# Filling TensorE's pauses with unread products, moving biases and a rank step, in a six-stage float32 kernel

## The chip, the cores and the metric

The kernel runs on one core of one Trainium2 chip. The core has a matrix engine (TensorE, PE in the profile; its weight loads are PEld), a vector engine (DVE), a scalar engine (ACT), a general engine (POOL), and SP, which here issues DMAs. Each engine works through its own queue of instructions in order; engines wait for each other on semaphores. TensorE writes its products to PSUM, the other data lie in SBUF.

The metric is device time in microseconds. Before the change it is 1187.05 us, the median of three runs (1184.86 to 1189.95).

## The reference, cut to what matters

`x` is 2 x 64 x 1024 (128 rows, one for each SBUF partition); six stages each add their result to it, and each but the first stage's context reads a layer norm of `x`.

```python
x = x + xattn0(layernorm(x), ctx)      # q1 = fake_quant(x1), q2 = fake_quant(ctx); q1 @ q2
x = x + mamba(layernorm(x), ...)       # in_proj, causal conv of 4, SSM over 8 groups of 16 heads, gate, group RMS norm, out_proj
x = x + lora_ffn(layernorm(x), ...)    # base product + top-2 of 8 LoRA experts
x = x + graph(ctx, layernorm(x), ...)  # four space-filling orders of the points, windows of 10 neighbours, attention, two layers, conv3
x = x + (layernorm(x) @ (weight * block_mask).T)
x12 = layernorm(x) @ w12.T + b12       # the last stage
x1, x2 = split(x12, 2)
x = x + (silu(x1) * x2) @ w3.T + b3
```

The graph stage takes its points from the context (the first three features of 1024 positions). To sort them, four keys are made for each point (Morton and Hilbert order, each with the axes in two orders), and each point's rank among the 1024 keys is counted.

## The kernel before

All is written out as one program; the loops are Python loops.

**Attention and state-space stage** (`mamba`). `quant_attention` (L171) loads the context in four pieces, quantizes and multiplies them. The function's last step is handed back as `update`, which the layer norm (`layernorm`, L140) applies to each half of `x`. `transposed` (L156) turns the normed `h` into `hT` with eight TensorE transposes (L163), copied out by DVE for the first half and ACT for the second. From there `project` (L312 to L320) multiplies `hT` by chunks of `in_proj_w`: a load of up to four chunks (2 MB) on SP into one of three buffers, then 8 products a chunk (L319) into one of two PSUM tiles of pool `pin`.

The order of instructions on all engines is the order in which the code is written (`manual_schedule`). For each of eight groups `g` the loop (from L464) does: two projections of the main path, each followed by `conv` (ACT L325 and L328, DVE L334, ACT L335); two projections of the gate; in the second of them `decays` (products L384 and L392 in pool `ps`, two buffers, tag `misc`; DVE `gm` L386 and `mt` L396, ACT L395); `turned` (transposes L405, DVE `xs` L406); the first half of the out projection of the group before (`out_half`, L453); `mixed` (L417); the other half; `gated` (DVE L429 to L436), `accumulate` (L461). `rms` of a group (L440) stands behind the next group's first projection.

Between these, `side(n)` runs the next n steps of `point_ranks`, a generator that makes the sorting keys and ranks, mostly on DVE. Steps of its Hilbert loop (L635 to L650) are 17 small integer operations each; later steps are the comparisons L724 and L725. Group 0 runs one step after each of its two `conv` and two after each gate projection; groups from 1 on also run two after the first `out_half` and four after `accumulate`.

**LoRA stage** (`lora_experts`). A layer norm with the last group's `update`, transposes, the router product L524, the base product L528, then the experts; L566 is the last product.

**Graph stage** (`point_cloud`). Its preparation is not in a hand-written order. It loads small weights on SP (L760 to L766 for each of two layers), the biases of the last stage (L1083, L1084), the spread and the masked linear's weight `w_attn` (4 MB, L1253). Then an iteration for each of 88 sets of points, with PSUM pools `g_ps` (3 buffers of tag `misc`), `g_pa` (2, `sc`), `g_po` (2, `op`) and `g_pt` (1, `pt`): one PSUM bank each, eight in all. At its end conv3 (L1187) is summed in two `op` tiles, normed (L1200 to L1208), passed through a leaky ReLU (for the second half POOL L1210 makes 0.2 h, DVE L1214 takes the larger), and added to `x` (L1212, L1215).

**Last stage** (`masked_linear_and_ffn`). It opens PSUM pools of its own: four tiles `p12`, two `lo`, two `misc`. Four bias products (L1272: a row of 6 biases chosen by a column of the identity, 6 rows deep) start `p12`; then norm, transposes (`turn`, L1282), the masked linear into `lo` (L1276, 32 records of 512 columns), the sum with `x` (L1309), norm and transposes again, two bias products into new `lo` tiles, four products with w12 (64 records), ACT's SiLU (L1319) and DVE's product (L1321), transposes, and the product with w3 in two halves (2 x 16 records). The weights (three loads of 4 MB, L1266 and L1268) go out on SP when the graph stage's SBUF comes free. A float32 product appears as two records of TensorE.

Of the kernel before, what the change touches and what calls it, by code (L numbers as in the profile page):

```python
# [14 lines left out]
AF = mybir.ActivationFunctionType  # L15
ALU = mybir.AluOpType
# [4 lines left out]
P = 128  # L21
D = 1024
# [70 lines left out]
class Kernel:  # L93
# [46 lines left out]
    def layernorm(self, pool, tag="h", update=None):  # L140
# [13 lines left out]
        return h  # L154

    def transposed(self, pool, ps, h, tag="hT"):  # L156

        nc = self.nc
        hT = self.t(pool, [P, KC, P], tag=tag)
        for q in range(2):  # L160
            pt = self.t(ps, [P, 4, P], tag="misc")
            for j in range(4):
                nc.tensor.transpose(pt[:, j, :], h[:, (4 * q + j) * P:(4 * q + j + 1) * P], self.ident)  # L163
            if q == 0:
                nc.vector.tensor_copy(hT[:, 0:4, :], pt)
            else:
                nc.scalar.copy(hT[:, 4:8, :], pt)
        return hT
# [106 lines left out]
    def mamba(self):  # L275
# [3 lines left out]
        with ExitStack() as es:  # L279
# [7 lines left out]
            convw, convb, normw = self.convw, self.convb, self.normw  # L287

            h = self.layernorm(sb, update=update)
            hT = self.transposed(sb, ps, h)  # L290
# [13 lines left out]
            def side(n):  # L304
                for _ in range(n):
                    next(pieces, None)
# [157 lines left out]
            for g in range(G):  # L464
                cs, h0 = grp(g)
                st = dict(xc=self.t(gp, [P, CPG, P], tag="xc"), sg=self.t(gp, [P, CPG, P], tag="sg"), rl=[])
                for q in range(2):
                    rl = self.t(hp, [P, 8, S], tag="rl")
                    nc.gpsimd.tensor_tensor(rl, cm.unsqueeze(1).to_broadcast([P, 8, S]),
                                            dtT[:, 1, h0 + 8 * q:h0 + 8 * q + 8].unsqueeze(2).to_broadcast([P, 8, S]), ALU.mult)  # L470
                    st["rl"].append(rl)
                for q in range(2):
                    pt = project(17 + 16 * g + 4 * q, 4)
                    if q == 0 and prev:
                        rms(g - 1, prev)
                    conv(st["xc"][:, 4 * q:4 * q + 4, :], pt, CPG * g + 4 * q)
                    side(1)
                for q in range(2):
                    pt = project(25 + 16 * g + 4 * q, 4)
                    if q:  # L480
                        decays(g, st)
                    settle()
                    nc.scalar.activation(st["sg"][:, 4 * q:4 * q + 4, :], pt, AF.Silu)
                    side(2)
                if g == G - 2:
                    nc.sync.dma_start(self.w_ra, a["router_lora_a"])
                    nc.sync.dma_start(self.w_lb, a["lora_B"])
                turned(g, st)
                if prev:
                    out_half(g - 1, prev, 0)  # L490
                    side(2)
                mixed(g, st)
                if prev:
                    out_half(g - 1, prev, 1)
                gated(g, st)
                if prev:
                    accumulate(g - 1, prev)
                    side(4)
                prev = st
# [12 lines left out]
            def update(q, c):  # L512
                nc.vector.scalar_tensor_tensor(self.x[:, c], prev["po"][:, q, :], prev["rs"], self.x[:, c], ALU.mult, ALU.add)

            self.lora_experts(sb, ps, pout, update)

# [544 lines left out]
    def point_cloud(self):  # L1061
        nc, tc, a = self.nc, self.tc, self.a
        with ExitStack() as es:
            pool = lambda n, b, **k: es.enter_context(tc.tile_pool(name=n, bufs=b, **k))
            self.g_ps, self.g_pa = pool("g_ps", 3, space=PSUM), pool("g_pa", 2, space=PSUM)
# [15 lines left out]

            self.bias = self.t(self.g_win, [6, 512], tag="bias", bufs=1)
            nc.sync.dma_start(self.bias[0:4, :], a["L1_ffn_b12"].rearrange("a (q n) -> (a q) n", n=512))  # L1083
            nc.sync.dma_start(self.bias[4:6, :], a["L1_ffn_b3"].rearrange("a (q n) -> (a q) n", n=512))  # L1084
            self.ident16 = self.t(self.g_w, [P, P], BF16, tag="ident16")
# [100 lines left out]
            def part(q, r, w, v, start=False, stop=False):  # L1186
                nc.tensor.matmul(po[q][r, :], w, v[:, 512 * q:512 * q + 512], start=start, stop=stop, skip_group_check=True)  # L1187
# [8 lines left out]
            for q in range(2):  # L1196
                part(q, hi, w3b, phases[3]["out"], stop=True)
            st = self.t(self.g_hm, [P, 2, 6], tag="st3")
            for q in range(2):
# [9 lines left out]
            t3 = self.t(self.g_hm, [P, 512], tag="f11")  # L1209
            nc.gpsimd.tensor_scalar(t3, h[1], 0.2, None, ALU.mult)  # L1210
            nc.vector.scalar_tensor_tensor(h[0], h[0], 0.2, h[0], ALU.mult, ALU.max)
# [42 lines left out]


    def masked_linear_and_ffn(self):

        nc, tc, a = self.nc, self.tc, self.a
        with ExitStack() as es:
            sb = es.enter_context(tc.tile_pool(name="l_sb", bufs=1))  # L1260
            pp = es.enter_context(tc.tile_pool(name="l_po", bufs=1, space=PSUM))
            ps = es.enter_context(tc.tile_pool(name="l_ps", bufs=2, space=PSUM))
            es.enter_context(tc.manual_schedule(engines=ENGINES))
# [6 lines left out]

            def biased(po, j):
                nc.tensor.matmul(po, self.ident[0:6, j:j + 1].to_broadcast([6, P]), self.bias, start=True, stop=False)  # L1272

            def product(po, hT, w, n, kcs, biased):
# [3 lines left out]
            def turn(v, n):  # L1278

                pt = self.t(ps, [P, 4, P], tag="misc")  # L1280
                for j in range(4):
# [17 lines left out]

            p12 = [self.t(pp, [P, 512], tag=f"p12{j}") for j in range(4)]  # L1300
            for j in range(4):
                biased(p12[j], j)
            hT = normed(self.st)
            st = self.t(sb, [P, 2, 6], tag="st5")
            po = [self.t(pp, [P, 512], tag=f"lo{n}") for n in range(2)]
            for n in range(2):
                product(po[n], hT, self.w_attn, n, range(KC), False)
            for n in range(2):
                nc.vector.tensor_tensor(half(self.x, n), half(self.x, n), po[n], ALU.add)  # L1309
                nc.vector.bn_stats(st[:, n, :], half(self.x, n))  # L1310
            hT = normed(st)
            po = [self.t(pp, [P, 512], tag=f"lo{n}") for n in range(2)]
            for n in range(2):
                biased(po[n], 4 + n)
            act = self.t(sb, [P, D], tag="act")
# [7 lines left out]
            for n in range(2):  # L1323
                product(po[n], aT, w_3, n, range(4), True)
            aT.append(turn(act, 1))
            for n in range(2):
                product(po[n], aT, w_3, n, range(4, KC), True)
            for n in range(2):
# [67 lines left out]
```

## Time and profile before

| | |
|---|---|
| median of three runs | 1187.05 us (1184.86 to 1189.95) |
| the profiled execution | 1189.64 us, of which the span from first to last instruction is 1187.9 us |
| mean granted TensorE clock | 0.942 |
| DMA | 170.89 MB, mean 144 GB/s |
| stretch before the first projection, 41.62 to 47.77 us | PE busy 0.00 us |
| between `turned` and `mixed` of group 0, 116.34 to 122.90 us | PE busy 0.00 us |
| before the router, 484.92 to 490.60 us | PE busy 0.00 us |
| preparation of the graph stage, 512.24 to 554.20 us | PE busy 9.52 us |
| graph loop, 554.20 to 1102.06 us | PE busy 487.83 us |
| last stage from 1102.06 us | 85.8 us |

A profile is one execution taken by the hardware profiler. "Busy" is time in which an engine works on an instruction; for TensorE the clock that was granted (1.00 is full) is recorded as well. A wait names the instruction that waited, what released it, the total, how often, and the longest. In forty slices of 29.7 us each, the clock that TensorE was granted (in tenths, 9 is 0.9 or more) and the DMA engines' share:

```profile
PEclk9899899999999998875998989898999999999889
DMA  7777468686695757556011003010222000000640
```

The slices below full clock are spread over the run; the DMAs work mainly until 490 us, and again near the end.

### The profile page before, as it was taken

The numbers are of one execution on the slowest core, as the hardware profiler recorded it, in microseconds if no ns is written. First come the engines' busy times: TensorE is split into PE (matmuls) and PEld (weight loads), VectorE is DVE, ScalarE is ACT, GpSimd is POOL, SyncE is SP. The second block draws the span as 40 slices with busy tenths as digits, with TensorE's granted clock in tenths as the row PEclk, the third lists the DMA queues.
The fourth block names the chain that finished last, engine by engine and source line by source line (L and its number), as shares of the span: only waits on it lengthen the run. The fifth ranks groups of instructions, "written<-read, shape, count | busy, mean of one in ns | idle before, by whom it ended". The sixth has DMA issues, their size and how long they took to land.

```text
span 1187.9 us, 40798 instructions
## 1 busy us (share of the span) xinstructions
PE 1034.0 (87%) x18349; PEld 790.4 (67%) x18349; DVE 736.6 (62%) x1545; ACT 656.5 (55%) x1056; POOL 497.8 (42%) x404
## 2 busy tenths in 40 slices
PE   4699899999999998743887888888999989999998
PEld 1598869769678693432665666667778767777333
DVE  5688775767666755442554666666767568986311
ACT  4443326565664561014886788776777676776010
POOL 0010110101325145337877877685757658841000
PEclk9899899999999998875998989898999999999889
DMA  7777468686695757556011003010222000000640
GB/s 258 288 289 278 194 277 354 248 355 272 241 417 198 328 231 227 185 200 93 14 23 25 15 12 66 17 35 9 39 37 38 10 11 11 10 4 3 244 180 18
DMA packets 47888, 170.89 MB, mean 144 GB/s; under 512 B 26409, under 2 KB 27349, under 8 KB 40801
## 3 DMA queue, kind: packets, MB, share of 16 engines
q1 hardware_dynamic: 37704, 151.22, 34.3%
q10 hardware_dynamic: 3864, 12.82, 3.2%
q0 software_dynamic: 6144, 4.24, 1.9%
q8 instruction: 144, 2.36, 0.8%
q14 instruction: 32, 0.25, 0.1%
HBM read 163.05 MB, written 2.72 MB: 140 GB/s over the span
## 4 chain that ended last, share of the span: by engine, by line
PE 57%; DVE 18%; ACT 9%; issue 6%; POOL 6%; DMA 3%; SPq 1%; another core or an unknown queue 0%; ACTq 0%; DVEq 0%; POOLq 0%
PE misc L953 12%; PE pin L319 11%; PE po L453 7%; PE op L968 5%; DVE cpre L334 3%; PE sc L918 3%; POOL x L886 3%; ACT df L725 3%; PE p L1276 3%; PE lo L1276 2%; PE pt L978 2%; DVE df L724 2%; POOL e L936 2%; PE sc L927 1%; DMA ow<-in_ctx 1%
## 5 line engine op out<-in xcount | busy, mean ns | idle before, releaser
L319 PEld LDWEIGHTS pin<-hT,w 128*128 128x128 f32 x2320 | 264.6, 194 | 3.5 <-issue 3.0
L319 PE MATMUL pin<-hT,w 128*128 128x128 f32 x2320 | 266.4, 278 | 0.1
L953 PE MATMUL misc<-wz,xz 128*64 128x64 bf16 (+1 forms) x8256 | 211.2, 212 | 13.7 <-issue 9.6
L953 PEld LDWEIGHTS <-xz 128*64 128x64 f16 x8256 | 196.4, 115 | 30.5 <-issue 26.8
L886 POOL TENSOR_TENSOR x<-win,cen 128x960 f16<-128x960 f32 x88 | 171.0, 1949 | 66.3 <-PE sc L918 31.1
L955 ACT COPY u<-misc 128x512 f32<-128x512 f32 x258 | 148.8, 587 | 54.8 <-PE misc L953 29.3
L854 POOL DMA_INDIRECT sl<-src,place x128 | 129.0, 1007 | 44.7 <-issue 18.7
L909 ACT COPY xz<-x 64x1024 f16<-64x1024 f16 (+1 forms) x132 | 134.7, 1020 | 6.4 <-POOL x L886 3.4
L940 DVE STREAM_TRANSPOSE at<-e 128x512 f32<-128x512 f32 x88 | 61.4, 698 | 110.1 <-POOL e L936 110.0
L433 POOL TENSOR_TENSOR xc<-y,normw 128x512 f32<-128x512 f32 x8 | 8.3, 1038 | 279.7 <-DVE y L431 230.5
L936 POOL TENSOR_TENSOR e<-e,z 128x512 f32<-128x512 f32 x88 | 94.5, 1074 | 71.7 <-DVE z L935 63.8
L725 ACT ACTIVATE df<-df,neg 128x1024 f32<-128x1024 f32 x64 | 73.4, 1147 | 89.8 <-DVE df L724 85.3
L453 PE MATMUL po<-ow,xc 128*128 128x512 f32 x256 | 115.4, 604 | 1.9 <-DVE acc L461 1.4
L968 PE MATMUL op<-u,at 128*32 128x64 f32 (+1 forms) x2752 | 93.8, 255 | 22.3 <-issue 13.4
L334 DVE SCALAR_TENSOR_TENSOR cpre<-craw,convw,cpre 128x126 f32<-128x126 f32 (+2 forms) x240 | 78.1, 347 | 29.1 <-ACT cpre L328 23.4
L968 PEld LDWEIGHTS op<-u,at 128*32 128x32 f32 x2752 | 64.5, 112 | 39.8 <-issue 21.8
L918 PEld LDWEIGHTS <-xz 128*64 128x64 f16 x2752 | 54.6, 113 | 49.1 <-issue 48.4
L453 PEld LDWEIGHTS po<-ow,xc 128*128 128x128 f32 x256 | 48.1, 193 | 58.1 <-issue 55.4
L724 DVE SCALAR_TENSOR_TENSOR df<-hi_r,hl,lo_r 128x1024 f32<-128x1024 f32 x64 | 81.7, 1303 | 4.0 <-DMA lo_r<-rows 2.8
L708 POOL DMA_INDIRECT place<-cst,rank x64 | 66.1, 1033 | 40.1 <-issue 15.3
L918 PE MATMUL sc<-x,xz 128*64 128x32 f16 x2752 | 66.6, 186 | 6.4 <-issue 6.4
L970 ACT COPY oT<-op 128x256 f32<-128x256 f32 (+1 forms) x88 | 41.4, 471 | 54.4 <-PE op L968 48.4
(319 smaller groups left out, 1400.3 us busy)
## 6 DMA issues: line engine op xcount, KB each, us to landing
w<-in_in_proj_w SPq DMA_DIRECT2D x36, 2048.0 KB
ow<-in_out_proj_w SPq DMA_DIRECT2D x16, 2048.0 KB
w<-in_L_ffn_w SPq DMA_DIRECT2D x3, 4096.0 KB
ow<-in_ctx SPq DMA_DIRECT2D x8, 1024.0 KB
hi_r<-rows ACTq DMA_DIRECT2D x8, 512.0 KB
lo_r<-rows ACTq DMA_DIRECT2D x8, 512.0 KB
df<-in_L_attn_mask ACTq DMA_DIRECT2D x8, 512.0 KB
w<-in_base_W SPq DMA_DIRECT2D x2, 2048.0 KB
```

The lines of the kernel that those rows point to most:

```text
L319: nc.tensor.matmul(pt[:, c, :], w[:, c, kc, :], hT[:, kc, :], start=(kc == 0), stop=(kc == KC - 1))
L334: nc.vector.scalar_tensor_tensor(pv[:, :, s:], rv[:, :, :S - s], convw[:, cc + c, 3 - s:4 - s], pv[:, :, s:], ALU.mult, ALU.add)
L453: nc.tensor.matmul(st["po"][:, n, :], st["xc"][:, 4 * q + c, :], ow[:, c, 512 * n:512 * n + 512], start=(q == 0 and c == 0), stop=(q == 1 ...
L725: nc.scalar.activation(df, df, AF.Sign, bias=neg[:, cc:cc + 1], scale=1.0, accum_out=sums[:, c:c + 1])
L854: nc.gpsimd.indirect_dma_start(out=ph[c][:, m, :], out_offset=None, in_=ph["src"][:, :], in_offset=bass.IndirectOffsetOnAxis(ap=k, axis=0))
L886: nc.gpsimd.tensor_tensor(xv, over, mid, ALU.subtract)
L909: nc.scalar.copy(dst, src)
L918: nc.tensor.matmul(sc[64 * hp:64 * hp + 64, k, :], xz[:, hp, k].rearrange("p a j -> p (a j)"), x[:, hp, k, :], start=False, stop=False, sk ...
L936: nc.gpsimd.tensor_tensor(e, e, z.unsqueeze(2).to_broadcast([P, nb, 32]), ALU.mult)
L953: nc.tensor.matmul(pu[64 * hp:64 * hp + 64, k, :], xz[:, hp, k0 + k].rearrange("p a j -> p (a j)"), wz[j][:, hp, :], start=(j == 0), stop= ...
L955: nc.scalar.copy(u[:, k0:k0 + kb], pu)
L968: nc.tensor.matmul(op[32 * r:32 * r + 32, q, :], it["at"][:, 4 * q + r, :], it["u"][:, 4 * q + r, :], start=False, stop=True, skip_group_c ...
```

## The change

- A new function `filled` issues n products of the identity with the first 256 columns of the constants into a PSUM tile that nobody reads.
- It is called four times: 11 products after the attention's last one, before the layer norm of the state-space stage; 11 before the LoRA stage's layer norm; 10 at the end of the graph stage, after conv3 and two bias products; 2 in the last stage, after the masked linear and the other two bias products.
- In group 0 the two rank steps after the second gate projection move behind `gated`.
- The graph stage's PSUM pools stay open to the end of the kernel, and the last stage uses their tiles: `p12` are three `misc` and one `pt`, `lo` are `sc`, the transposes `op`. The last stage's own PSUM pools are gone.
- The bias products for w12 (now 4 rows deep) are issued in two pairs: behind conv3, and behind the masked linear.
- The bias of w3 is no longer a product: it is loaded to all 128 partitions (512 KB) and added to `x` on DVE after the second norm.
- The scaling by 0.2 at the end of the graph stage moves from POOL to ACT.

```diff
+    def filled(self, pt, n):
+        for _ in range(n):
+            self.nc.tensor.matmul(pt[:, 0:256], self.ident, self.cst[:, 0:256], start=True, stop=True)
...
+            self.filled(self.t(pin, [P, 512], tag="pin"), 11)
             h = self.layernorm(sb, update=update)
             hT = self.transposed(sb, ps, h)
...
                     nc.scalar.activation(st["sg"][:, 4 * q:4 * q + 4, :], pt, AF.Silu)
-                    side(2)
+                    side(2 if prev or q == 0 else 0)
...
                 gated(g, st)
                 if prev:
                     accumulate(g - 1, prev)
-                    side(4)
+                side(4 if prev else 2)
...
+            self.filled(self.t(pin, [P, 512], tag="pin"), 11)
             self.lora_experts(sb, ps, pout, update)
...
-            pool = lambda n, b, **k: es.enter_context(tc.tile_pool(name=n, bufs=b, **k))
+            pool = lambda n, b, **k: (self.ctx if k.get("space") is PSUM else es).enter_context(tc.tile_pool(name=n, bufs=b, **k))
...
-            self.bias = self.t(self.g_win, [6, 512], tag="bias", bufs=1)
-            nc.sync.dma_start(self.bias[0:4, :], a["L1_ffn_b12"].rearrange("a (q n) -> (a q) n", n=512))
-            nc.sync.dma_start(self.bias[4:6, :], a["L1_ffn_b3"].rearrange("a (q n) -> (a q) n", n=512))
+            self.bias = self.t(self.g_win, [4, 512], tag="bias", bufs=1)
+            nc.sync.dma_start(self.bias, a["L1_ffn_b12"].rearrange("a (q n) -> (a q) n", n=512))
+            self.bias3 = self.t(self.g_win, [P, D], tag="bias3", bufs=1)
+            nc.sync.dma_start(self.bias3, a["L1_ffn_b3"].rearrange("a n -> (a n)").partition_broadcast(P))
...
                 part(q, hi, w3b, phases[3]["out"], stop=True)
+            self.p12 = [self.t(self.g_ps, [P, 512], tag="misc") for _ in range(3)] + [self.t(self.g_pt, [P, 512], tag="pt")]
+            for j in range(2):
+                self.biased(j)
+            self.lo = [self.t(self.g_pa, [P, 512], tag="sc") for _ in range(2)]
+            self.filled(self.lo[0], 10)
...
-            nc.gpsimd.tensor_scalar(t3, h[1], 0.2, None, ALU.mult)
+            nc.scalar.activation(t3, h[1], AF.Identity, scale=0.2)
...
+    def biased(self, j):
+        self.nc.tensor.matmul(self.p12[j], self.ident[0:4, j:j + 1].to_broadcast([4, P]), self.bias, start=True, stop=False)
...
-            p12 = [self.t(pp, [P, 512], tag=f"p12{j}") for j in range(4)]
-            for j in range(4):
-                biased(p12[j], j)
+            p12, po = self.p12, self.lo
             hT = normed(self.st)
...
                 product(po[n], hT, self.w_attn, n, range(KC), False)
+            for j in range(2, 4):
+                self.biased(j)
+            po = [self.t(self.g_pa, [P, 512], tag="sc") for n in range(2)]
+            self.filled(po[0], 2)
...
             hT = normed(st)
-            po = [self.t(pp, [P, 512], tag=f"lo{n}") for n in range(2)]
-            for n in range(2):
-                biased(po[n], 4 + n)
+            nc.vector.tensor_tensor(self.x, self.x, self.bias3, ALU.add)
...
-                product(po[n], aT, w_3, n, range(4), True)
+                product(po[n], aT, w_3, n, range(4), False)
```

## The prediction

> **What bounds the kernel now.** I read the page's shares and chain first, then the waits of PE stretch by stretch, then the clock.
>
> ```profile
> PE 1034.0 (87%) x18349; PEld 790.4 (67%) x18349; DVE 736.6 (62%) x1545; ACT 656.5 (55%) x1056; POOL 497.8 (42%) x404
> ...
> PE 57%; DVE 18%; ACT 9%; issue 6%; POOL 6%; DMA 3%; SPq 1%; another core or an unknown queue 0%; ACTq 0%; DVEq 0%; POOLq 0%
> ```
>
> PE is busy 87% and carries 57% of the chain of waits. It matters where it stands still, and how fast it runs afterwards. The waits of PE before 130 us, in 470 to 560 us, and after 1090 us:
>
> ```profile
> PE py L417 <- DVE xs L406: 6.6, 1, 6.6
> PE misc L163 <- issue: 6.2, 1, 6.2
> ```
> ```profile
> PE misc L770 <- DMA wv<-in_W_conv: 11.1, 1, 11.1
> PE misc L163 <- DVE h L153: 5.7, 1, 5.7
> ```
> ```profile
> PE misc L1282 <- DVE h L1295: 3.0, 1, 3.0
> PE p L1272 <- ACT f L1207: 2.7, 1, 2.7
> ```
>
> All but the DMA wait are touched by the change. Now the clock, in stretches cut where it turns (columns: stretch, length, busy us and count of PE, PEld, DVE, ACT and POOL, granted clock, DMA share, GB/s):
>
> ```profile
> 41.62:46.70 5.08, 0.00 (x0) 0.00 (x0) 4.28 (x6) 0.46 (x2) 0.00 (x0) 1.00 0.67 285
> 46.70:46.90 0.20, 0.00 (x0) 0.00 (x0) 0.00 (x0) 0.19 (x1) 0.00 (x0) 0.51 0.00 0
> 46.90:53.40 6.50, 5.63 (x25) 5.33 (x26) 2.35 (x8) 0.59 (x1) 0.00 (x0) 0.50 0.01 3
> ...
> 483.50:486.90 3.40, 1.41 (x5) 0.53 (x3) 1.92 (x4) 0.00 (x0) 2.17 (x3) 1.00 1.05 392
> ...
> 490.40:493.70 3.30, 3.10 (x13) 2.80 (x14) 1.21 (x3) 0.59 (x1) 0.96 (x1) 0.50 0.03 4
> ...
> 1104.95:1108.20 3.25, 3.25 (x4) 1.33 (x5) 3.15 (x5) 0.00 (x0) 1.72 (x1) 0.50 0.00 0
> 1108.20:1111.65 3.45, 3.45 (x5) 0.98 (x3) 2.25 (x6) 0.29 (x1) 0.00 (x0) 0.50 0.47 121
> ```
>
> After each pause PE runs at half clock: 46.70 to 53.53, 118.38 to 128.62, 487.02 to 493.85, 1104.83 to 1115.08, 1132.14 to 1142.38. Those lengths are 6.83 or 10.24 us: two or three times 3.413. Every turn lies on one grid of 3.413 us. On that grid the stretch before a fall had PE busy 20 to 39% and the one at 51% (39.87 to 43.29) did not fall; the stretch before a rise was busy 95% or more outside the graph stage. And 1104.95 to 1111.65 is busy throughout with bias products of 6 rows, yet the clock stays half: such products count for little.
>
> **Rule against row.** The Trainium skill, "TensorE: Matmul & The Clock Gate" (Why this matters for your kernels), allows idle gaps up to about 3 us. By it, every pause the fills leave is safe. The row 483.50:486.90 says otherwise: PE stopped at 484.90, and the clock fell at 487.02, 2.1 us later, because that grid stretch was only 38% busy. I go by the row; it costs 0.9 us below. Its Part 4 says that transposes don't count as busy. Row 490.40:493.70 is over half transposes (1.94 us), and the clock rose at its end: here they count. I take it that products with the identity count too; by Part 4's reading they might not (rival A).
>
> **One fill.** A product is two records (L319: 145 chunks x 8 make 2320). At full clock a 128-column record costs 7.14/64 = 0.112 us, a 512-column one 6.87/16 = 0.430. For 256 columns I take 0.218 (bounds 0.11 and 0.43): 11 fills 4.8 us, ten 4.4, two 0.9.
>
> **Part 1, fill before the first projection.** PE stops at 41.62, transposes start at 47.77 when h is there. The fill runs to 46.4, hidden by DVE's norm; 1.35 us stay open, so no stretch falls below 60%. The half clock goes: transposes to projection 1.37 us (as at 1131.43 to 1132.8) for 1.94, and L319's 3.82 us at half (49.71 to 53.53) do in 1.9. **-2.6.** The DVE chain that PE meets at 83.42 starts from this projection's end and moves along; weights are there (no DMA moved at 50 to 52).
>
> **Part 2, the rank piece.** In group 0 two rank steps (116.27 to 122.16, 5.9 us of DVE) stand between `mt` and `xs`. Without them `xs` starts at 116.4, L417 at 117.1 instead of 122.90, takes 1.15 for 1.99, and the next L319 x64 takes 7.14 for 9.14. PE is 8.6 us early. But the steps (34 DVE instructions, no DMA, nothing for SP or POOL) come back after `gated`. DVE then runs without a pause: `gated` 118.3 to 125.3, the steps to 131.2, then L444, convolutions and four steps (19.97 us from 135.48 to 155.45 now) to 151.4. There stands `gm` (L386), 156.00 now. PE reaches L384 at 147.0, but the second `misc` of L392 needs the buffer that `gm` frees: PE waits some 3.3 us. So -5.1 stays. Queued behind that wait are L405 and L453. The two steps after it still hide beneath L453's 6.87 us. A 3.3 us idle lets the clock fall in three of four positions of the grid, at some 2 us: 1.5. **-3.6** (bounds 0 and -5.1).
>
> **Part 3, fill before the router.** 484.92 to 489.7, h's transposes at 490.60. Transposes and L524 at full clock: L528 starts at 493.9 for 495.25. **-1.35.** The place loads are far ahead (needed at 508.98).
>
> **Part 4, the biases' loads.** Two small loads become one small and one of 512 KB, on SP at 512.5, ahead of `w_attn` (4 MB) and of layer 2's `wv`, which is issued at 518.80, lands at 527.36 and is what PE L770 waits for. All go through one queue. The nearest row is the pair of rank rows, 1 MB of broadcast at 340 to 350 GB/s (175 to 177 us): half of it is 1.5 us. Bounds 0 (no queueing) and 2.6 (half of the pair's 5.2 us from issue to use). Everything before the graph stage is behind it. **+1.4.** The graph loop has no edit; its PSUM pools only live longer.
>
> **Part 5, last stage.** Now the eight 6-row records begin at 1104.80, when the old pools come free, and last to 1111.9 at half clock; h would have allowed 1110.7. New: biases 0 and 1 at 1102.06 (4 x 0.43), ten fills to 1108.1. ACT takes POOL's scaling (0.59, like L1287, for 1.84); DVE never waited for it, but L1212 took 0.98 beside POOL and 0.69 alone: h 0.3 earlier, transposes at 1110.4, `lo` at 1111.8 for 1113.81, at full clock 13.7 for 14.6: over at 1125.5 for 1128.42. Then 2.3 + 0.7 us of DVE to the transposes at 1128.5; biases 2 and 3 and two fills take 2.6 of these 3.0. Those fills write the buffer of the first `lo`, so they and the transposes queued behind them wait for L1309's first half; it is read 6 us earlier, so that costs nothing. The four records for b3 (1132.76 to 1136.46) are gone: L1276 starts at 1129.9. Its 64 records take 27.5 for 30.6. The sum x + b3 is 1.2 us of DVE (like L502), idle there until the third product. Together **-9.6**. Next late could be the weights: their 12.6 MB flow from 1110 to 1141.2, w_3 being last and wanted at 1158: no. Risk: 2.3 us open before 1110.4 let the clock fall in near half the positions, at 1.6 us, and a little more at the second pause: +0.9. **-8.7.**
>
> **Sum.** -2.6 - 3.6 - 1.35 + 1.4 - 8.7 = -14.9. The profiled execution took 1189.64 (span 1187.9 and 1.7 around it), so 1174.8; the median shown is 1187.05, 2.6 lower, and I forecast against it: **1172**. Grid positions differ between executions, worth 2 to 3 us either way; with part 2's and part 4's bounds the likeliest case spans 1166 to 1178.
>
> **Rivals.**
> A: identity products don't hold the clock. For it: the 6-row bias products held nothing. Against: the transposes. The clock then falls within the fills, and they outlast their pauses: part 1 +0.6, part 3 +1.8 (2.7 us of fill left at 487.02 double), part 2 -3.6, part 4 +1.4, part 5 only the biases' move, -4.5: together -4.3, 1182.7, "same".
> B: the moved rank steps return the whole gain. PE's 3.3 us stall at L392 opens a long half-clock stretch and `xs` becomes late as well: part 2 is 0, giving 1175.8. For it: DVE has no slack from 118 to 154. Against: L453 hides 6.9 us behind it.
> C, slower: each fill record takes 0.43, as a 512-column one or at half clock from the start, and holds nothing. Then 11 fills take 9.5 us: +3.4 at 47.77, +3.8 at 490.60, ten end at 1114.2, +2.3; the small fill adds 2.2, part 4 1.4, against -3.6 and the -3.7 of b3: +5.8, 1193. It decides from about 0.35 us a record, where a fill outlives its pause. Against: the clock is 1.00 at the start of each pause, and the two measured widths lie on a line.
>
> **Chances.** Main 0.70, B 0.13, A 0.12, C 0.05. A measurement tells 0.5%, 5.9 us, from nothing. Main and B are faster; A lies at 0.4% and is split in favour of same. Range 1165 to 1180.
>
> **What would show it.** Clock 1.00 from 41 to 60 us, from 477 to 510 and from 1092 to the end; PE's wait at L417 gone, one of some 3 us at L392 in group 1; `wv` landing 16.5 us after the first bias load (15.1 now); L1272's second set gone and L1276 x64 at 27.5. I am wrong if half clock remains beneath the fills, if transposes start late behind them, or if the graph stage, 548 us with no edit, changes by over 3 us.

## The result and the profile after

The changed kernel took **1179.54 us**, the median of 7 runs (1169.95 to 1182.05), beside 1188.94 for 7 runs of the kernel before: a ratio of 0.9902, 95% interval 0.9879 to 0.9925. The forecast was 1172, range 1165 to 1180, "faster" at 0.85. The direction held, and so did the range, by half a microsecond at its upper end. The gain is 9.4 us where the sum said 14.9, and that it came so near is in part luck: two terms of the sum were wrong in opposite directions, as the table below shows.

First the page of the profile after, with the rows that answer to those shown of before: the shares of the engines, then the chain that ended last.

```profile
PE 1036.7 (88%) x18413; PEld 796.2 (68%) x18413; DVE 737.9 (63%) x1546; ACT 656.5 (56%) x1057; POOL 498.0 (42%) x403
...
PE 55%; DVE 22%; ACT 9%; issue 6%; POOL 4%; DMA 4%; SPq 0%; ACTq 0%; another core or an unknown queue 0%; DVEq 0%; POOLq 0%
```

PE has 64 more records and is busier by 2.7 us; the span went from 1187.9 to 1178.6 us and the mean granted clock from 0.942 to 0.956. Busy time says nothing about the gain here: added records were put where PE stood still. The waits of PE, in the same three parts of the run (total, times, longest):

```profile
PE misc L398 <- DVE gm L392: 3.2, 1, 3.2
...
PE misc L168 <- DVE h L153: 1.3, 1, 1.3
```
```profile
PE misc L777 <- DMA wv<-in_W_conv: 2.1, 1, 2.1
```
```profile
PE op L1294 <- issue: 2.2, 1, 2.2
```

The 6.6 us wait for `xs` is gone and one of 3.2 us for `gm` stands in group 1, as forecast. The 6.2 and 5.7 us before the norms' transposes are 1.3 and 0.95. The 11.1 us wait for `wv` is 2.1, which was not forecast. Now the clock, in stretches of the changed kernel (columns as before the prediction: PE, PEld, DVE, ACT and POOL busy, granted clock, DMA share, GB/s):

```profile
41.42:46.44 5.02, 5.02 (x23) 4.10 (x22) 4.28 (x6) 0.45 (x1) 0.00 (x0) 1.00 0.72 302
478.41:483.30 4.89, 4.89 (x23) 3.99 (x21) 4.34 (x9) 0.30 (x1) 2.53 (x4) 1.00 1.04 370
1102.31:1106.90 4.59, 4.58 (x21) 3.71 (x20) 4.42 (x7) 1.41 (x2) 0.00 (x0) 1.00 0.00 0
```
```profile
146.70:149.95 3.25, 0.33 (x2) 0.22 (x4) 2.77 (x15) 0.33 (x1) 0.00 (x0) 1.00 0.98 418
149.95:153.40 3.45, 3.45 (x13) 2.05 (x10) 1.69 (x5) 2.04 (x3) 0.00 (x0) 0.51 1.04 442
508.40:556.15 47.75, 18.40 (x304) 15.15 (x304) 14.01 (x43) 18.60 (x25) 24.77 (x20) 0.50 0.78 176
```

The first three rows are the fills: 22, 22 and 20 records at full clock (the counts of the rows take in one neighbour), 0.23 us each, and no half clock under or behind the first two. The next two are the wait for `gm` and the half clock that it leaves. The last row is the graph's opening, which lies at half clock throughout; before, 41.0 of the 44.4 us from 514.3 to 558.7 us did.

**Where the time went.** There are two profiles of each kernel, since the loop was a surprise. The table gives after minus before, in us, stage by stage (a negative number is a gain of that stage), for the first pair of profiles and for the second, with the mean beside the prediction's term.

| stage, up to | first pair | second pair | mean | predicted |
|---|---|---|---|---|
| `gm` product of group 0 (part 1) | -2.35 | -1.67 | -2.0 | -2.6 |
| `po` product of group 1, then the router's transposes (part 2) | -3.67, -0.31 | -3.95, +1.45 | -3.2 | -3.6 |
| end of the router's product, then LoRA's last product, L566 before and L573 after (part 3) | -1.11, 0.00 | -2.29, -0.20 | -1.8 | -1.35 |
| POOL's first edge operation (part 4) | -2.05 | -0.15 | -1.1 | +1.4 |
| end of the last conv3 product (graph loop) | +7.91 | +0.44 | +4.2 | 0 |
| end (part 5) | -7.63 | -7.56 | -7.6 | -8.7 |
| sum | -9.2 | -13.9 | -11.6 | -14.9 |

Two rows are off: the loads before the graph gained where I charged them, and the loop, which has no edit, gave back 4 us on average, 8 in the first pair and next to nothing in the second.

### The profile page after: what moved, and what is told of

The parts are those of the page before. It is cut to its first block, busy times and chain, and to the rows that moved or that the text cites. A ratio compares the mean times of both kernels' runs of the same rounds, so it can differ in the third digit from the quotient of the medians.

```text
span 1178.6 us, 40925 instructions
## 1 busy us (share of the span) xinstructions
PE 1036.7 (88%) x18413; PEld 796.2 (68%) x18413; DVE 737.9 (63%) x1546; ACT 656.5 (56%) x1057; POOL 498.0 (42%) x403
## 4 chain that ended last, share of the span: by engine, by line
PE 55%; DVE 22%; ACT 9%; issue 6%; POOL 4%; DMA 4%; SPq 0%; ACTq 0%; another core or an unknown queue 0%; DVEq 0%; POOLq 0%
PE misc L960 13%; PE pin L325 8%; PE po L459 7%; PE op L975 5%; DVE cpre L340 4%; PE sc L925 4%; ACT df L732 3%; PE pt L985 3%; PE sc L1288 2%; DVE df L731 2%; POOL x L893 2%; PE misc L1288 2%; PE sc L934 2%; POOL e L943 2%; PE op L972 1%
## 5 line engine op out<-in xcount | busy, mean ns | idle before, releaser
L325 PEld LDWEIGHTS pin<-hT,w 128*128 128x128 f32 x2320 | 260.9, 192 | 4.5 <-issue 3.8
L325 PE MATMUL pin<-hT,w 128*128 128x128 f32 x2320 | 263.0, 275 | 0.9 <-issue 0.4
L960 PEld LDWEIGHTS <-xz 128*64 128x64 f16 x8256 | 197.9, 115 | 34.4 <-issue 30.4
L893 POOL TENSOR_TENSOR x<-win,cen 128x960 f16<-128x960 f32 x88 | 170.7, 1946 | 73.0 <-PE sc L925 28.6
L459 PE MATMUL po<-ow,xc 128*128 128x512 f32 x256 | 115.3, 604 | 1.7 <-DVE acc L467 1.4
L340 DVE SCALAR_TENSOR_TENSOR cpre<-craw,convw,cpre 128x126 f32<-128x126 f32 (+2 forms) x240 | 78.2, 347 | 28.1 <-ACT cpre L334 20.1
L925 PEld LDWEIGHTS <-xz 128*64 128x64 f16 x2752 | 55.8, 115 | 52.4 <-issue 50.7
L459 PEld LDWEIGHTS po<-ow,xc 128*128 128x128 f32 x256 | 48.2, 193 | 57.8 <-issue 55.2
L941 DVE TENSOR_REDUCE z<-e 128x16 f32<-128x512 f32 x88 | 58.8, 668 | 22.3 <-ACT e L936 21.1
```

The source lines that it names most:

```text
L325: nc.tensor.matmul(pt[:, c, :], w[:, c, kc, :], hT[:, kc, :], start=(kc == 0), stop=(kc == KC - 1))
L340: nc.vector.scalar_tensor_tensor(pv[:, :, s:], rv[:, :, :S - s], convw[:, cc + c, 3 - s:4 - s], pv[:, :, s:], ALU.mult, ALU.add)
L459: nc.tensor.matmul(st["po"][:, n, :], st["xc"][:, 4 * q + c, :], ow[:, c, 512 * n:512 * n + 512], start=(q == 0 and c == 0), stop=(q == 1 ...
L893: nc.gpsimd.tensor_tensor(xv, over, mid, ALU.subtract)
L925: nc.tensor.matmul(sc[64 * hp:64 * hp + 64, k, :], xz[:, hp, k].rearrange("p a j -> p (a j)"), x[:, hp, k, :], start=False, stop=False, sk ...
L960: nc.tensor.matmul(pu[64 * hp:64 * hp + 64, k, :], xz[:, hp, k0 + k].rearrange("p a j -> p (a j)"), wz[j][:, hp, :], start=(j == 0), stop= ...
```

## The experiments

The theories. **T1**: the loop gives back what came before it, because it is entered earlier and cold, and more of it runs at half clock. **T2**: something in the loop became slower by itself (the 4 MB load of `w_attn` at its start, PSUM pools kept open). **T3**: chance; an execution falls on one of many positions of the 3.413 us grid, and the first pair was unlucky. "The loop" is counted from POOL's first edge operation (L893) to the end of the last conv3 product. An item is one of its 88 sets of points; a placing is the copy, the transposes (L871) and the copy back that bring gathered points into the tile `win`.

### Both kernels again

No edit.

> The changed kernel unaltered, for a second profile. The graph loop is counted from its first edge operation on POOL (L893) to the start of the last conv3 product (L1195). In the first profiles it took 555.4 us before, with 49.5 us at half clock, and 563.3 after, with 63.2 us. Theory T1 (the loop gives back what came before it because more of it runs at half clock): the loop takes 531 us plus half of its half-clock time, within 1.5 us, in this profile too. Rival T2 (something in the loop has become slower by itself: the 4 MB load of w_attn at its start, the PSUM pools kept open): the loop takes 562 us or more whatever its half-clock time. Rival T3 (chance: the profile of after caught an unlucky position on the 3.413 us grid): the loop takes about 556 here and the median falls to 1173-1176. T1 and T2 expect a median of 1178-1181.

> The kernel before unaltered, for a second profile. T1: the loop, counted as in the other runs, takes 531 us plus half of its half-clock time, within 1.5 us. T2: 555 us within 1.5, whatever the half clock. T3: the half-clock time in the loop differs from the 49.5 us of the first profile by 5 us or more.

Measured: the changed kernel 1178.95 (6 runs), ratio 0.9906 [0.987, 0.9942]; the kernel before 1190.35 (22 runs). The changed kernel's loop took 559.0 us with 54.3 us of half clock (563.3 and 63.4 in its first profile), the one before 558.6 with 58.3 (555.4 and 49.6). T2's "562 or more whatever the half clock" is out. T1's formula (531 us and half of the half clock) gives 558.2 and 560.2, off by 0.8 and 1.6 where 1.5 was allowed; a narrow miss, and I kept it for now. That the open PSUM pools slow the loop was not tried by itself in any run. T3 is right in that half-clock time in the loop differs by 9 us between two executions of the same kernel, and so do 3 to 4 us of the loop; the median did not fall to T3's 1173 to 1176.

### The fills taken out

```
         for _ in range(n):      ->      for _ in range(0):
```

> The changed kernel with the four fills at zero records; the biases, the rank steps and the scaling stay as changed. By the prediction's parts the clock falls again at 46.7, 487 and in the last stage: +2.6, +1.35, and some 3.6 of part 5, so 1179.5 + 7.5 = 1187 if the graph loop keeps its length. T1: the graph stage is reached about 4 us later and the loop's front is half clock either way, so the loop is shorter by up to 4 us and the total is 1183 to 1187. T2: the loop stays at 563, total 1187. Rival A of the prediction (products with the identity hold no clock): 1179.5 within 1.

Measured: 1182.38 (17 runs), ratio 0.9934 [0.9914, 0.9954], so **the four fills are worth about 3.4 us** of the 11.6 that the changed kernel gains beside it (by the ratios, with both measurements of the changed kernel, 3.7 and an interval of 3.3 either way), not the 7.5 of the prediction's parts. That identity products hold the clock (against rival A) is plain in the profile: half clock is back at 44.6 to 51.5, 485.0 to 488.4, 1106.2 to 1113.0 and 1130.1 to 1133.5 us. But the first edge operation came at 539.1, no later than the changed kernel's 537.1 and 540.0: the 1.3 us of the first fill (L390 of group 0 at 111.70 for 110.44) are not seen in front of the graph any more. The last stage took 79.5 us from the last conv3 product, against 78.2 and 77.0 with fills and 85.8 and 84.5 before. There most of part 5 is the rest of the change, the biases' move above all (some 5.7 us, not taken apart further), and the fills add 1.9.

### The rank piece taken back

```
-                    side(2 if prev or q == 0 else 0)
+                    side(2)
...
-                side(4 if prev else 2)
+                if prev:
+                    side(4)
```

> The changed kernel with the rank steps back where they stood before; everything else as changed. Group 1's L459 should start 3.6 us later than in the changed kernel (part 2 of the prediction: -6.0 measured against -2.35 before it). T1: of these 3.6 us the loop gives back some or all, total 1179.5 to 1183. T2 and T3: all 3.6 arrive, 1183.

Measured: 1179.16 (13 runs), ratio 0.9914 [0.9889, 0.9938]; no difference to the changed kernel that can be seen. In the profile, L459 of group 1 starts at 156.12 for 152.99 and 152.40 (3.4 us later, as forecast); at the router's product 2.0 us of that are left on average (2.7 and 1.3 against the two profiles). The profiled loop was short, 557.4 us with 47.1 of half clock. The rank piece is worth 2 us at the router. At the end the ratios give it 1.3 us, with an interval of 3.7 either way.

### The load of w_attn out of the graph's way

```
-        return [lambda: nc.sync.dma_start(self.w_attn, ...
+        return [lambda: nc.scalar.dma_start(self.w_attn, ...
```

> The changed kernel with one edit: the 4 MB load of w_attn is issued on ACT's queue in the iteration it was planned for (item 68) and no longer stands ahead of the graph's own loads on SP's queue. In the changed kernel src is issued at 515.6 us and lands at 524; 4 MB at some 350 GB/s are 12 us. If src's landing bounds the graph's start, the first edge operation comes about 5 us earlier than in the changed kernel (537.1 and 540.0 in its two profiles), at 532 to 535. T1 and T3: the loop then gives back some of it, total 1174 to 1178 for 1179. T2 (the load of w_attn slows the loop's first part): all of it and more arrives, 1171 to 1174.

On ACT's queue the load goes out at 962.1 us. Measured: **1172.85** (6 runs), ratio 0.9844 [0.9812, 0.9876]: 6 us faster than the changed kernel by the medians, and clear of noise by the ratios (7 us, with an interval of 4.5 either way). The waits of POOL in 500 to 560 us, of the changed kernel and then of this one:

```profile
POOL sl L861 <- DMA src<-fT: 13.6, 1, 13.6
```
```profile
POOL sl L861 <- DMA src<-fT: 8.7, 1, 8.7
```

POOL's first gather reads `src`, and `src` is what the graph waits for. Issued at 515.6 us behind `w_attn` it let POOL start at 524.5; without that load ahead it was issued at 518.7 and POOL started at 522.6: 8.9 us against 3.9. Whether `src` lost this by its place in the queue or by sharing the DMA engines with the 4 MB was not separated. From LoRA's last product to the first edge operation the changed kernel needs 34.4 and 35.9 us, this one 28.6. The kernel before needs 36.5 and 36.0, and POOL's wait there was the longest:

```profile
POOL sl L854 <- DMA src<-fT: 17.8, 1, 17.8
```

There the reason was another. SP's issue of `src`, before and in the changed kernel, and what SP waited for in the kernel before:

```profile
532.19 0.39 SPq L800 DMA_DIRECT2D src<-fT  x1
515.64 0.38 SPq L807 DMA_DIRECT2D src<-fT  x1
```
```profile
SPq L800 <- DVE fT L798: 3.8, 1, 3.8
```

Before, `src` went out when `w_attn` had long been loaded, and POOL started 3.9 us later. It went out late because `fT` was late: DVE's copy L772 waited 8.1 us for the product L770, which waited for `wv`, and `fT` stands behind it. So the wait for `wv` did hold the entry before. In the changed kernel SP issues `wv` at 506.2, ahead of the 512 KB bias (506.9) and of `w_attn` (509.9); PE's 11.1 us wait became 2.1, and `src` goes out 13 us after LoRA's last product begins, for 22 before. Of these 9 us, 5 are lost again as `src` lands behind the 4 MB, and 2 more behind the gathers, where POOL waits some 3 us for ACT's `win`; 1.1 us reach the first edge operation on average. That is where the sign of part 4 went wrong.

### The opening kept warm, in two tries

```
             def iteration(i):
+                n = {-2: 54, 0: 20}.get(i)          # second try: {-2: 30, -1: 3, 0: 8}
+                if n:
+                    self.filled(self.t(self.g_po, [P, 512], tag="op"), n)
```

> The changed kernel with 74 more fill records in the graph's opening (540 to 560 us stage): 54 from the layer weights' products to the second placing's transposes, 20 before the first item's scores; PE sits idle there for 16 and 6 us and the clock is at half from 508 to 556. T1: the clock rises at about 525 and stays, so items 0 to 4, which run at half clock in the changed kernel, go faster: the loop's half-clock time falls from 54-63 us to about 46, the loop takes 2 to 4 us less (about 555 to 557), total 1175.5 to 1177.5. T3 (position alone): the loop's opening gains under 1 us since POOL and ACT set its pace, total 1178 to 1180.

Measured: 1178.26 (6 runs), ratio 0.9892 [0.9852, 0.9932]. I had mis-sized it: a product is two records, and I had counted it as one. The fills outlived their pauses, as the timeline of PE shows (start, us, what, idle before):

```profile
540.28 0.69 PE L871 MATMUL misc<-cst,pm 128*128 128x128 f32 x2 [4.03 <-ACT pm L868]
540.76 4.56 PE L159 MATMUL op<-cst 128*128 128x256 f32 x14
545.15 0.38 PE L871 MATMUL misc<-cst,pm 128*128 128x128 f32 x2
545.37 8.80 PE L159 MATMUL op<-cst 128*128 128x256 f32 x40
554.01 0.38 PE L922 MATMUL sc<-mask,ident 128*128 128x512 bf16 x1
```

PE reaches the first item's scores at 554 us, behind 8.8 us of fill. So this try cannot judge T1, and the second was sized by it, on top of the late load.

> The kernel of the run before with w_attn's load late, and 41 fill products (82 records) in the graph's opening. The first try of this had 74 products, and a product is two records, so its fills overran their pauses by up to 9 us and the opening came 1.5 us late and took 3.3 us longer. Here 30 of them are due before the first placing's transposes (some 8 us of a pause of 10), 4 between the two placings, 9 before the first item's scores (3.5 of 4.8 us). T1 (the clock is what the loop's opening costs): with full clock in items 0 to 4, the stretch from item 0 to item 8 takes 37 to 38 us for the 39.9 of that run, total 1169 to 1171 for 1172.9. Rival (POOL, ACT and DVE set the pace of the opening, half clock there costs nothing): 39.5 to 40.5 us from item 0 to item 8, total 1171.5 to 1174, with about 100 us of half clock falling to 65.

Measured: 1174.02 (6 runs), ratio 0.9848 [0.9805, 0.9891], for 0.9844 without these fills. The stretch from item 0 to item 8 in the kernel with the late load, and in this one:

```profile
534.40:574.30 39.90, 29.02 (x996) 22.63 (x996) 18.59 (x40) 31.07 (x45) 32.41 (x26) 0.82 0.22 34
```
```profile
531.80:571.40 39.60, 32.41 (x1017) 25.24 (x1015) 18.58 (x40) 30.98 (x45) 32.39 (x26) 0.96 0.24 37
```

The clock went from 0.82 to 0.96 and the stretch from 39.9 to 39.6 us. POOL is busy 32.4 us of it and ACT 31.0 in both. **T1's cold entry falls**: the half clock of the opening, the largest block of it in the profile, costs next to nothing. From LoRA's last product to the first edge operation it is 28.1 us for 28.6. The next run has the same fills here, and it took 28.3 and 40.2 us, so the gain is within what two profiles differ by.

### The last stage's fill longer

```
-            self.filled(self.lo[0], 10)
+            self.filled(self.lo[0], 13)
```

> As e3_late_front, and the fill of the last stage is 13 products long for 10, so the 2.2 us that PE stands before its first transposes shrink to 0.8. The clock fell there in four of seven profiles of kernels with 10 (2.2 us after the last record; the last stage took 78.8 to 79.2 us where it fell and 77.6 where it didn't). Expected: no half clock in the last stage in its profile, which takes 77.6 us, total 0.5 to 1 us under e3_late_front. If the longer fill delays the transposes: 78.5 or more.

Measured: 1170.48 (6 runs), ratio 0.9823 [0.9789, 0.9857]. At the first pause of the last stage the clock held, as expected, but it fell at the second (1117.0 to 1120.4), and the stage took 78.2 us. PE was busy 3.37 of 3.41 us just before that fall; some 2 us of this were the 4-row bias products, which count for little, as those of 6 rows did before. With the shorter fill, in e3_late_front, it held at both and the stage took 76.9. The intervals of the two ratios overlap: nothing is shown for the longer fill.

### The rank piece, a second time and pushed further

> The kernel with w_attn's load late, and the rank steps back where they stood before the change. By the prediction's part 2 the first edge operation comes 3.6 us later (534.4 with the steps moved) and so does the end: 1176.5. If the gain of the rank piece is lost inside the loop whatever happens at its start, as in the pair without the late load (1179.2 and 1179.0): 1173.

The edit is the one above, on the kernel with the late load. Measured: 1171.09 (6 runs), ratio 0.9819 [0.9785, 0.9854], against 0.9844 with the steps moved. The first edge operation came at 535.2 for 534.4, where 3.6 us more were expected. Again no loss can be seen; both comparisons together give 0 us, with an interval of 3 either way.

Pushed further, two rank steps of group 1 move as well, from its first gate projection to behind `accumulate`:

```
                     settle() ...
-                    side(2 if prev or q == 0 else 0)
+                    side(0 if q == (g == 0) and g < 2 else 2)
...
-                side(4 if prev else 2)
+                side((2, 6)[g] if g < 2 else 4)
```

> The changed kernel with two more rank steps of group 1 moved from its first gate to behind accumulate, so that gm of group 1 is in time. The 3.2 us wait of PE for gm and the half-clock stretch from 150 us disappear, L459 of group 1 starts 4 to 5 us earlier (152.4 to 153.0 now). Theory: that gain goes the way of the first rank piece, which measured 0 in total (1179.2 without it, 1179.0 with it): total 1177 to 1179. Rival: it arrives, 1174.5.

Measured: 1194.27 (22 runs), ratio 1.0019 [1.0001, 1.0037]. Slower than the changed kernel by 15 us, which neither side expected. L459 of group 1 came at 148.54, 4 us earlier, as planned. Then, in 160 to 200 us, the waits of DVE, and of PE in 140 to 215 us:

```profile
DVE df L731 <- DMA lo_r<-rows: 20.0, 1, 20.0
```
```profile
PE pin L325 <- ACT craw L331: 16.2, 1, 16.2
```

Six steps in a row reach the point at which the rank piece stores its keys as `rows` in DRAM and reads them back, spread over the partitions, as `hi_r` and `lo_r`. With other work between the steps that trip is hidden; with none DVE stands 20 us, the convolutions queue behind it, and PE's buffers stay full. It shows how little separates a moved step that costs nothing from rival B's picture.

### A pure delay at the loop's door

```
-                    self.edges(it)
+                    for _ in range(3 if i == 0 else 1):      # 5 in the second
+                        self.edges(it)
```

The first edge operation is repeated with the same result.

> The changed kernel with a pure delay at the loop's door: POOL's first edge operation (1.96 us, its output the same each time) is done three times, so everything after it comes 4.1 us later. It asks what an arrival a few us earlier or later is worth at the end, with nothing else changed. If an arrival counts in full: 1179 + 4.1 = 1183. If the loop gives back arrivals of this size (the reading of the rank piece, whose 3 us at the first edge were not found in the totals: 1179.2 against 1179.0, 1171.1 against 1172.9): 1178 to 1180.5.

> As e4_delay2, with the first edge operation done five times, 8.2 us of delay, so that the loop begins about where it begins in the kernel before. If an arrival counts in full: 1187. If the loop gives back arrivals: 1179 to 1183. If it begins where the kernel before does and its time were set by its position alone, its half-clock time would be that of before, 50 to 58 us; by chance of the grid, anything from 47 to 63.

Measured: 1182.56 (7 runs), ratio 0.9927 [0.99, 0.9955], and 1189.33 (22 runs), ratio 0.9982 [0.9966, 0.9997]. Against the changed kernel the planned delays of 4.1 and 8.2 us (3.8 and 8.9 at the second item's edge operation) cost 2.8 and 9.4 us by the ratios, with intervals of 4 and 3 either way. The longer one counts in full; the shorter is not told from nothing. So the loop does not give back 8 us, and T1 falls in its other half too for arrivals of that size. For 2 to 4 us, the size of the rank piece, these runs cannot say.

### What the loop's time does follow

Fourteen profiles of twelve kernels have the same order of instructions in the loop after its opening, except for one load and, with the late load, a few placings around item 68. From the ninth edge operation on, their loops take 513.1 to 524.1 us and hold 27 to 55 us of half clock. A straight line through them is 503.0 us plus 0.375 us for each us of half clock, with a correlation of 0.83; the slope is known to 0.16 either way, and single profiles, which come from more than one chip, lie up to 4.3 us off the line. Some stretches by item, each as length and half clock in us:

| items | before | before again | after | after again | rank taken back | late load, rank taken back | delay 8.2 |
|---|---|---|---|---|---|---|---|
| 22 to 24 | 10.0, 0 | 10.0, 0 | 11.1, 0 | 10.8, 0 | 10.8, 0 | 11.2, 0 | 11.0, 0 |
| 40 to 45 | 27.2, 5 | 27.5, 5 | 29.6, 10 | 28.8, 7 | 26.9, 3 | 25.9, 0 | 29.4, 10 |
| 45 to 66 | 137.2, 7 | 137.6, 7 | 138.7, 10 | 138.3, 7 | 137.9, 7 | 138.1, 7 | 138.3, 7 |

At items 40 to 45 the third phase begins and PE waits for placings; whether the clock falls there, once, twice or not at all, makes 25.9 to 29.6 us of the same work. I read that as chance of the grid position, T3: the two executions of the changed kernel differ there too, 10 and 7 us of half clock with the same program.

There is also a piece that is not the clock. By that slope the two profiles of before hold 502 us without half clock, and six of the changed kernel's kind with `w_attn` on SP 505, while two more of this kind (the first warm opening, the rank piece pushed further) have 503 and the four with the late load 499 to 503. At items 22 to 24 I can see one part of it, 0.8 to 1.2 us in the table. Of the seven profiles not shown there, six have 10.8 to 11.6 us, and the one with the longer fill has 10.0, as before. These are rows of PE's timeline there, in the kernel before and in the one with the rank piece taken back:

```profile
665.74 1.71 PE L953 MATMUL misc<-wz,xz 128*64 128x64 bf16 x96
```
```profile
660.29 1.51 PE L961 MATMUL misc<-wz,xz 128*64 128x64 bf16 x83
662.08 0.41 PE L961 MATMUL misc<-wz,xz 128*64 128x64 bf16 x13 [0.27 <-issue]
```

Before, 96 products run through in 1.71 us; after, the same 96 have a pause in them in which PE waited for nothing that the profile shows. The products behind them start 0.5 us later, counted from the first of the 96, and POOL's next edge operation 0.8. Such pauses are in all these profiles, 50 to 61 of them between 560 and 1085 us, 25 to 28 us together. In the changed program they stand at other products, though the order of the instructions there is the same. Why they stand where they do was not tried, and the remaining 2 us or so stay open.

## Why the prediction came out as it did

**Part 1, -2.6; measured -2.0.** Right in kind and nearly in size; the two items that the part lists come to 2.5, not 2.6. Transposes start at 47.71 and run at full clock.

**Part 2, -3.6; measured -3.2 at the router.** PE's wait at L398 was foreseen (3.3, measured 3.2 us), and so was the half clock behind it. The gain shrinks on its way to the router, and the totals show none of it, within some 3 us. Rival B, that the steps return the whole, is nearer to the totals than I gave it, though not by a cold `xs`.

**Part 3, -1.35; measured -1.8.** Right, though taking all the fills out delayed the graph's entry by nothing that the profile shows.

**Part 4, +1.4; measured -1.1.** The sign was wrong. The step that failed is "on SP at 512.5, ahead of `w_attn` (4 MB) and of layer 2's `wv`". The order of SP's loads was not that of before: `wv` went ahead of the new bias load and of `w_attn`. The wait for `wv` that the term was taken from was real, since `fT` and so `src` stood behind it; it went away, and `src`, now issued 9 us earlier, met the 4 MB load and POOL's later wait instead. So 1.1 us were gained where 1.4 had been charged.

**Part 5, -8.7; measured -7.6.** Here the risk of 0.9 came true in the first profile and not in the second. The gap of 2.2 us before the transposes was foreseen at 2.3. On the grid of 3.413 us, the stretch that holds it, in the changed kernel's first profile and in its second:

```profile
1105.70:1109.11 3.41, 1.22 (x7) 0.77 (x6) 2.72 (x7) 0.29 (x1) 0.00 (x0) 1.00 0.25 55
1109.11:1112.52 3.41, 3.41 (x10) 2.33 (x11) 0.81 (x2) 0.58 (x1) 0.00 (x0) 0.50 1.00 407
```
```profile
1106.29:1109.70 3.41, 1.71 (x10) 1.26 (x11) 1.86 (x4) 0.85 (x2) 0.00 (x0) 1.00 0.83 281
```

Busy 36% of a grid stretch, and the next ran at 0.50; busy 50%, and it stayed at 1.00. The gap was 2.2 us long both times. The Trainium skill, "TensorE: Matmul & The Clock Gate" (Why this matters for your kernels), calls gaps up to about 3 us safe; this one of 2.2 us was not, and by these rows the share of the grid stretch decides, which is a matter of position.

The share alone decides only at its ends. In all fourteen traces, from 30 us on and each cut on its own grid, the clock fell behind 73 of 73 full-clock stretches that were busy under 40%, behind 50 of 64 at 40 to 50%, 30 of 87 at 50 to 60%, 19 of 148 at 60 to 70%, 6 of 347 at 70 to 80%, and 1 of 3560 at 80% or more, the one with the 4-row bias products above. So the "20 to 39%" of the prediction is too narrow: the stretch from 43.29 to 46.70 us of the kernel before, busy 0, fell too, and in the graph stage stretches busy up to 67% did.

**The loop, 0; measured +7.9 and +0.4.** "The graph loop has no edit" is true and was not enough. I had named it as what would prove me wrong (over 3 us) and set 2 to 3 us for grid positions "either way". The loop alone varies by 3 to 4 us between two executions of the same kernel, and a shift of 2 to 3 us on average, which I had no term for and whose cause is open, lies on top. This is the term that was mis-sized: with the loop at +4.2 and part 4 at -1.1 the same sum gives some -13, against the -11.6 of two pairs.

**The rivals.** A falls: without the fills the clock falls in four places. C falls: a fill record took 0.23 us, not 0.43.

**A better version.** Four kernels with `w_attn`'s load late lie at 0.9819 to 0.9848 of the kernel before, and the one with that edit alone at 0.9844 [0.9812, 0.9876], where the changed kernel has 0.9902 [0.9879, 0.9925] and 0.9906 [0.987, 0.9942]. Which of the others is best the intervals do not tell. By the medians, one word on one load is worth more (6 us) than the four fills together (3.4).

## What to carry to other kernels

In this kernel a pause of TensorE cost what the work behind it lost at half clock, where TensorE set the pace, and next to nothing in the graph's opening, whose length stayed when the half clock went: fill the pauses ahead of dense products first. Before a fill is written, follow each queue that feeds the next stage to its first consumer on any engine; a 4 MB load that nothing reads for 480 us stood ahead of 256 KB on which the next stage waited, and PE's own waits did not name it. And a loop without an edit is not a constant: two profiles of each kernel are the least from which a stage's time may be compared when effects are of a few us.

## What the runs showed of the hardware

- Fills of identity products hold full clock (1.00 in all three rows); a record of 256 columns takes 0.23 us (22 in 5.02 us), and one fp32 product is two records.
- Some 31 us of half clock ahead of and inside the graph's opening (37.6 to 6.8, up to item 8) could be removed for a gain of 0.8 us in one profile (0.5 ahead of the first edge operation, 0.3 behind it) and none in the next.
- In the loop a us of half clock goes with some 0.375 us more (0.22 to 0.53). The half that a stage would lose if TensorE set its pace throughout is not excluded.
- Bias products of 4 rows count for little: PE was busy 3.37 of 3.41 us with some 2 us of them (1113.6 to 1117.0 us, the longer fill), and the clock fell.
- TensorE pauses 50 to 61 times in 525 us of the loop, mostly for 0.3 to 0.5 us, while it waits for nothing that the profile shows; the places change with the program though the order of the loop's instructions stays.
